# Reordering constants, weight loads and a flag in a graph kernel: three small moves on one Trainium2 core

## The chip, the cores and the metric

The kernel runs on one NeuronCore of a Trainium2 chip. The metric is the device time of one execution in microseconds (us). Below, TensorE is PE in profile lines (PEld its weight loads), VectorE is DVE, ScalarE is ACT, GpSimd is POOL, and SyncE is SP, whose queue (SPq) issues most transfers.

## The reference

The input is 16 graphs of 1024 nodes with 128 features, a 0/1 adjacency matrix for each, and a node mask of ones. Two layers are computed, each followed by a residual addition and a layer norm over the features. The first is a gated graph network (four steps of a GRU cell). The second first thins out each adjacency matrix row by row ("dilation"), then applies three rounds of neighbourhood averaging with batch norm, and a linear map of the three results:

```python
adj_d = _dilate(adj, mask)
def _sage(x, adj, Wr, Wx, b, mf):
    deg = jnp.clip(jnp.sum(adj, axis=-1, keepdims=True), 1.0, None)
    agg = jnp.einsum('bij,bjd->bid', adj, x) / deg
    out = agg @ Wr + x @ Wx + b
    return out / jnp.maximum(norm(out), 1e-12) * mf
h1 = _bn(relu(_sage(x,  adj_d, Wr1, Wx1, b1, mf)), g1, be1)
h2 = _bn(relu(_sage(h1, adj_d, Wr2, Wx2, b2, mf)), g2, be2)
h3 = _bn(relu(_sage(h2, adj_d, Wr3, Wx3, b3, mf)), g3, be3)
x = _layernorm(x + (concat([h1, h2, h3]) @ Wl + bl))
```

The batch norm takes its mean and variance over all graphs and nodes, so that each round has to be finished for all 16 graphs before the next one starts.

## The kernel before

The work stands in stages, and the order inside each stage is written out by hand: every engine runs its instructions in the order of the program, and semaphores join the engines.

From 0 to about 1330 us the GRU and the dilation run interleaved (`Gated` with lines L1062 to L1122, `FixPoint` with L735 to L912). The dilation is computed by a fixed number of sweeps instead of row by row; a check adds up, in the tile `bad`, whether that was enough and whether the inputs are what the fast path takes (0/1 values). At the very end `flagged` (L1954) reduces `bad` to one integer: VectorE takes the maximum over the columns, a matmul adds the partitions, and every engine loads the result into a register (`values_load`, L1967). If it is not zero, a general version of the whole computation runs (`tc.If`, L2007); with these inputs it is jumped over.

The first pass, `first` (L1415), takes the graphs one after the other in turns of 16 steps. `slot(b, t)` (L1600) is step t of the turn of graph b; in it the adjacency of graph b + 1 is already prepared. So there is a lead-in turn, b = -1, which only prepares graph 0. In a step, `unit` (L1474) turns one 128 x 512 piece of the thinned adjacency with matmuls (L1482, L1488, L1489) that read the loaded adjacency `p_a` and the removed entries `p_nr`; ScalarE writes the result to `p_at` (L1490), GpSimd packs it to bytes (`pack`, L1497) for the later passes, and VectorE checks the raw rows (`check`, L1506). `agg` (L1561) multiplies the features by `p_at`. `out_first` (L1570) applies the weights.

What the change moves in this pass:

- `load_given` (L1243) issues 20 transfers on the SP queue: six weight matrices and `Wl`, ten rows of vectors, the node mask three times. It is called at L1443, after the loads of graph 0 (two of `p_nr`, one of `p_s`, eight of `p_a`) and before the loop, so before the loads of graph 1, which `slot` issues at steps 4 to 11 of the lead-in turn: `p_nr` at 4 and 6, `p_s` at 7, the first four `p_a` tiles at 8 to 11. At step 10 the bytes of graph 0 are stored to `s_at`, after `pack` has written them. The transfers of the SP queue use eight semaphores in rotation, and an issue waits until the transfer eight places earlier has landed.
- `constants` (L1259), at step 9 of the lead-in turn, prepares small tiles on VectorE, among them `drop` (the identity with a changed first row) in the work tile `p_rl`, and a block of ones that three transfers store to `rho` (L1290).
- `first_weights` (L1293), at step 1 of the turn of graph 0, multiplies the first weight matrix by `drop`, turns the vectors and computes the bias row `s_r`, with PSUM tiles that TensorE writes and VectorE reads in alternation.

The second pass `second` (L1698) and the third pass `third` (L1830) compute rounds two and three from what the earlier pass stored. The third pass has 32 units (16 graphs, two halves) in a pipeline: in iteration i TensorE turns the rows of unit i - 3 (L1411), computes unit i (`out_next`, L1758, L1761, L1764), and VectorE and ScalarE scale and normalise the units in between.

`last` (L1867) adds the third linear map (L1890 to L1898) and does the final layer norm for each graph: eight tiles `u_y` of 128 x 128 are scaled and shifted, the first on GpSimd (L1921), the others on ScalarE (L1925), reading PSUM for tiles 4 to 7. For the last graph, VectorE takes tiles 2, 4 and 6 (L1923). Each graph is stored by one transfer of 512 KB on the SP queue (L1926).

Of the kernel before, what the change touches and what calls it, by code (L numbers as in the profile page):

```python
# [8 lines left out]
F32 = mybir.dt.float32  # L9
BF = mybir.dt.bfloat16  # L10
F16 = mybir.dt.float16
FR = mybir.dt.float32r
I32 = mybir.dt.int32
U8 = mybir.dt.uint8
AF = mybir.ActivationFunctionType
ALU = mybir.AluOpType
AX = mybir.AxisListType
# [4 lines left out]
P = 128  # L22
# [19 lines left out]
def rows_of(ap):  # L42

    return ap.rearrange("(k p) c -> p k c", p=P)
# [1152 lines left out]
class Sage:  # L1197
# [61 lines left out]
    def constants(self):  # L1259
# [16 lines left out]
        nc.vector.memset(self.r6[:, C:], 0.0)  # L1276
        work = self.wk.tile([P, NB, C], F32, name="p_rl", bufs=1)

        mask, junk = self.cst["mask"], work[:, 0, :].rearrange("p (a b) -> p a b", a=NB)
        nc.vector.scalar_tensor_tensor(junk, mask, 0.0, mask, op0=ALU.is_gt, op1=ALU.not_equal,  # L1280
                                       accum_out=self.bad[:, BAD - 1:BAD])

        drop = work[:, 1, :]
        nc.vector.tensor_copy(drop, ident)
        nc.vector.memset(drop[:1, :], -1.0)
        nc.vector.memset(drop[:1, :1], 0.0)
        o = work[:B, 4:, :].bitcast(BF).rearrange("p a b -> p (a b)")
        nc.vector.memset(o, 1.0)
        for i in range(3):
            nc.sync.dma_start(self.rho[:, 3 + i, :], o)  # L1290
        self.drop = drop

    def first_weights(self):  # L1293
        nc, ident = self.nc, self.cst["ident"]
        bank = lambda: self.ps1.tile([P, 4, P], F32, name="s_tr")[:, 0, :]
        w = bank()
        nc.tensor.matmul(w, self.drop, self.wr[:, 0, :], start=True, stop=True)
        nc.vector.tensor_copy(self.wr[:, 0, :], w)
        v = bank()[:, :10]
        nc.tensor.transpose(v, self.vr, ident[:10, :10])  # L1300
        nc.vector.tensor_copy(self.vt, v)
        self.weights(0, bank()[:6, :])
        nc.vector.tensor_copy(self.mask48, self.m48)
# [111 lines left out]
    def first(self):  # L1415

        nc, tc, cst = self.nc, self.tc, self.cst
        with ExitStack() as c:
# [22 lines left out]
            for k in range(4, NB):  # L1441
                self.load_a(0, k)
            self.load_given()  # L1443
            self.eps = self.const([P, 1], 1e-5, "s_eps")
# [4 lines left out]
            for t, v in ((self.xh, 1.0), (self.xl, 0.0)):  # L1449
                nc.vector.memset(t[:, :, :1].bitcast(F32), v)  # L1450
            for b in range(-1, B):
                for t in range(16):
                    self.slot(b, t)
# [146 lines left out]
    def slot(self, b, t):  # L1600
# [82 lines left out]
        if nxt:  # L1683
            if t == 10:
                nc.sync.dma_start(self.at8[n, 0], self.g[n]["b", 0])
            if t == 13:
                nc.sync.dma_start(self.x1[n], self.g[n]["s"])
        if (b, t) == (-1, 9):
            self.constants()
        if (b, t) == (0, 1):  # L1690
            self.first_weights()
# [138 lines left out]
    def third(self):  # L1830

        nc, tc = self.nc, self.tc
        with ExitStack() as c:
# [9 lines left out]
            units = [(b, f) for b in range(B) for f in range(2)]  # L1843
            for i in range(len(units) + 3):

                if i >= 3:
# [20 lines left out]
    def last(self, r48):  # L1867
        nc, tc, cst = self.nc, self.tc, self.cst
        with ExitStack() as c:
# [42 lines left out]
            def norm(b):  # L1912
                y, pp, mv, rs = st.pop(b)
                nc.vector.reciprocal(rs[:, 0, :], rs[:, 0, :])
                nc.vector.scalar_tensor_tensor(rs[:, 1, :], mv[:, :, 0], -1.0, rs[:, 0, :],
                                               op0=ALU.mult, op1=ALU.mult)
                for k in range(NB):
                    src = pp[:, k - 4, :] if k > 3 else y[:, k, :]
                    scale, shift = rs[:, 0, k:k + 1], rs[:, 1, k:k + 1]
                    if k == 0:  # L1920
                        nc.gpsimd.tensor_scalar(y[:, k, :], src, scale, shift, op0=ALU.mult, op1=ALU.add)  # L1921
                    elif b == B - 1 and k % 2 == 0:
                        nc.vector.tensor_scalar(y[:, k, :], src, scale, shift, op0=ALU.mult, op1=ALU.add)  # L1923
                    else:
                        nc.scalar.activation(y[:, k, :], src, AF.Identity, bias=shift, scale=scale)  # L1925
                nc.sync.dma_start(rows_of(self.out[b]), y)  # L1926

# [25 lines left out]

def flagged(tc, one, bad):  # L1954

    nc = tc.nc
    with tc.tile_pool(name="l_wk", bufs=1) as wk, tc.tile_pool(name="l_ps", bufs=1, space=PSUM) as ps:
        t = wk.tile([P, 1], F32, name="l_max")
        nc.vector.tensor_reduce(t, bad, axis=AX.X, op=ALU.max)
        nc.vector.tensor_scalar(t, t, 0.0, None, op0=ALU.not_equal)  # L1960
        col = wk.tile([P, 1], F32, name="l_col")
        nc.vector.memset(col, 1.0)
        pt = ps.tile([P, 1], F32, name="l_sum")
        nc.tensor.matmul(pt[:1], t, col, start=True, stop=True)
        f = one.tile([1, 1], I32, name="l_flag")
        nc.vector.tensor_scalar(f, pt[:1], 0.5, None, op0=ALU.is_gt)
    return nc.values_load(f[0:1, 0:1], min_val=0, max_val=1,  # L1967
                          skip_runtime_bounds_check_because="0 or 1 by is_gt")

# [19 lines left out]
def kernel(ctx: ExitStack, tc: tile.TileContext, x, adj, nodemask,  # L1989
# [7 lines left out]
    with ExitStack() as ctx:  # L1997
# [3 lines left out]
        with ExitStack() as c:  # L2001
# [3 lines left out]
            gru.run(fix.steps())  # L2005
        Sage(ctx, tc, cst, adj, not_r, summed, nodemask, W, vec, Wl, bl, out, bad).run()
    with tc.If(flagged(tc, one, bad) > 0):  # L2007
        general(tc, cst, x, adj, nodemask, weight, w_ih, w_hh, b_ih, b_hh, W, vec, Wl, bl, out)
# [31 lines left out]
```

## Time and profile before

| | |
|---|---|
| time, median of 3 runs | 2375.27 us (2373.47 to 2375.73) |
| span of the profiled execution | 2371.7 us |
| busy: PE, DVE, ACT, POOL | 2262.0 (95%), 1908.9 (80%), 1373.6 (58%), 1022.1 (43%) us |
| GRU and dilation | 0 to about 1330 us |
| first pass | about 1330 to 1870 us, 31 us a graph once it runs |
| third pass | about 2160 to 2282 us, 3.79 us a unit |
| last stage | about 2295 to 2362 us, then 9 us to the end of the span |

How to read it: the share of busy time is an average over stages. A TensorE that is busy 95% of the span is full in most stages, and the question for a change is in which stretch it stands, and for what. The timeline gives for each instruction its start, its duration, its engine and line, the tiles it writes and reads, and in brackets how long its engine was idle before it and what released it.

### The profile page before, as it was taken

The numbers are of one execution on the slowest core, as the hardware profiler recorded it, in microseconds if no ns is written. First come the engines' busy times: TensorE is split into PE (matmuls) and PEld (weight loads), VectorE is DVE, ScalarE is ACT, GpSimd is POOL, SyncE is SP. The second block draws the span as 40 slices with busy tenths as digits, with TensorE's granted clock in tenths as the row PEclk, the third lists the DMA queues.
The fourth block names the chain that finished last, engine by engine and source line by source line (L and its number), as shares of the span: only waits on it lengthen the run. The fifth ranks groups of instructions, "written<-read, shape, count | busy, mean of one in ns | idle before, by whom it ended". The sixth has DMA issues, their size and how long they took to land.

```text
span 2371.7 us, 35696 instructions
## 1 busy us (share of the span) xinstructions
PE 2262.0 (95%) x11929; PEld 1558.3 (66%) x11945; DVE 1908.9 (80%) x4130; ACT 1373.6 (58%) x3209; POOL 1022.1 (43%) x963
## 2 busy tenths in 40 slices
PE   6999999999999999999999699999999989999987
PEld 4665565666655656556566477777777768887865
DVE  4898998998989989989889877777777566665876
ACT  3656565656465655556564556656665545555756
POOL 3335254253362452533532446666666434441002
PEclk9999999999999999999999899999999999999999
DMA  7327245363353372543740677787778367774414
GB/s 263 112 97 263 72 163 177 115 216 129 119 201 108 115 248 68 198 142 115 234 133 25 236 279 274 270 297 278 273 272 298 116 237 247 246 247 157 138 43 135
DMA packets 214389, 436.17 MB, mean 184 GB/s; under 512 B 59570, under 2 KB 80724, under 8 KB 214196
## 3 DMA queue, kind: packets, MB, share of 16 engines
q1 hardware_dynamic: 186756, 345.96, 42.3%
q0 software_dynamic: 23040, 83.90, 10.4%
q10 hardware_dynamic: 4400, 3.95, 0.5%
q8 instruction: 96, 1.57, 0.3%
q14 instruction: 97, 0.79, 0.1%
HBM read 324.49 MB, written 109.25 MB: 183 GB/s over the span
## 4 chain that ended last, share of the span: by engine, by line
PE 63%; DVE 14%; DMA 8%; ACT 8%; issue 3%; POOL 3%; SPq 0%; DVEq 0%; ACTq 0%; POOLq 0%
PE h_g L1092 15%; PE h_g L1080 12%; PE p_ag L1561 9%; PE q_ag L1797 5%; PE q_ob L1764 3%; DVE f_rank L735 3%; DMA e_sum<-h_x 3%; PE p_u L1488 2%; PE p_u L1489 2%; DMA h_a<-in_adj_dram 2%; PE p_u L1482 2%; PE s_tr L1411 2%; ACT s_junk L1389 2%; PE q_oa L1758 2%; PE u_p L1890 1%
## 5 line engine op out<-in xcount | busy, mean ns | idle before, releaser
L1092 PE MATMUL h_g<-h_h,h_wh 128*128 128x512 f32 x768 | 397.7, 599 | 3.4 <-DVE h_r L1105 3.3
L1092 PE MATMUL h_g<-h_ms,h_wi 128*128 128x512 f32 x768 | 392.1, 592 | 0.0
L1497 POOL CAST p_b<-p_at 128x512 uint8<-128x512 f32 x256 | 252.5, 1006 | 137.5 <-ACT p_at L1490 129.5
L735 DVE TENSOR_TENSOR_SCAN f_rank<-f_a,f_first,f_pd 128x1024 f16<-128x1024 f32 x128 | 299.1, 2342 | 3.3
L1080 PE MATMUL h_g<-h_a,h_hi 128*128 128x512 f32 x1024 | 284.6, 418 | 6.6 <-DMA h_a<-in_adj_dram 6.6
L1490 ACT ACTIVATE p_at<-p_u,s_less 128x512 fp32r<-128x512 f32 x256 | 175.9, 688 | 157.5 <-PE p_u L1489 152.7
L1092 PEld LDWEIGHTS h_g<-h_ms,h_wi 128*128 128x128 f32 x768 | 145.6, 190 | 183.9 <-issue 161.6
L1121 POOL TENSOR_TENSOR h_h<-h_zh,h_r 128x512 f32<-128x512 f32 x126 | 181.9, 1443 | 194.9 <-DVE h_r L1120 172.8
L1080 PE MATMUL h_g<-h_a,h_lo 128*128 128x512 f32 x1024 | 264.2, 395 | 0.0
L1080 PEld LDWEIGHTS h_g<-h_a,h_hi 128*128 128x128 f32 x1024 | 188.4, 188 | 71.2 <-issue 20.1
L863 DVE SCALAR_TENSOR_TENSOR f_nr<-f_u,f_q,f_a 128x1024 bf16<-128x1024 f16 x128 | 184.0, 1454 | 56.9 <-ACT f_u L912 50.4
L1115 POOL TENSOR_TENSOR h_zh<-h_z,h_h 128x512 f32<-128x512 f32 x63 | 80.3, 1275 | 323.8 <-ACT h_z L1111 323.8
L1080 PEld LDWEIGHTS h_g<-h_a,h_lo 128*128 128x128 f32 x1024 | 190.0, 188 | 39.3
L1506 DVE SCALAR_TENSOR_TENSOR p_a<-p_a 128x1024 bf16<-128x1024 f32 x128 | 209.4, 1674 | 2.5 <-DMA p_a<-in_adj_dram 2.5
L1389 ACT ACTIVATE s_junk<-s_o 128x128 bf16<-128x128 f32 x384 | 113.8, 298 | 133.1 <-DVE s_o L1382 133.1
L1092 PEld LDWEIGHTS h_g<-h_h,h_wh 128*128 128x128 f32 x768 | 129.1, 190 | 86.6 <-issue 67.3
L1083 ACT COPY h_ms<-h_g 128x512 f32<-128x512 f32 x128 | 73.8, 577 | 175.4 <-PE h_g L1080 131.5
L1108 ACT ACTIVATE h_r<-h_r,h_bi 128x512 f32<-128x512 f32 x128 | 92.3, 721 | 138.5 <-DVE h_r L1107 138.5
L1488 PE MATMUL p_u<-ident_b,p_a 128*128 128x128 bf16 x1024 | 144.4, 221 | 13.8 <-DMA p_a<-in_adj_dram 12.8
L909 ACT ACTIVATE f_u<-f_rank,f_q 128x128 f16<-128x128 f16 (+7 forms) x128 | 110.6, 867 | 74.7 <-DVE f_rank L849 74.7
L1489 PE MATMUL p_u<-ident_b,p_nr 128*128 128x128 bf16 x1024 | 144.5, 221 | 0.0
L1764 PE MATMUL q_ob<-s_wxp,q_xt 128*128 128x256 f32 x512 | 130.5, 399 | 0.0
(258 smaller groups left out, 4936.0 us busy)
## 6 DMA issues: line engine op xcount, KB each, us to landing
h_a<-in_adj_dram POOLq DMA_DIRECT2D x128, 512.0 KB, 7.4
p_a<-in_adj_dram SPq DMA_DIRECT2D x128, 512.0 KB
f_a<-in_adj_dram SPq DMA_DIRECT2D x124, 512.0 KB
e_nr<-f_nr SPq DMA_DIRECT2D x128, 256.0 KB
p_nr<-e_nr SPq DMA_DIRECT2D x32, 1024.0 KB
s_at<-p_b SPq DMA_DIRECT2D x32, 512.0 KB
s_ag<-s_ag SPq DMA_DIRECT2D x64, 256.0 KB
q_agi<-s_ag SPq DMA_DIRECT2D x32, 512.0 KB
```

The source lines that it names most:

```text
L735: nc.vector.tensor_tensor_scan(out, a, other[:, 0, 0:1].to_broadcast([P, N]), start, op0=ALU.add, op1=ALU.bypass)
L863: nc.vector.scalar_tensor_tensor(nr, self.us[g], self.q[:, 2, g:g + 1], self.a[g], op0=ALU.not_equal, op1=ALU.is_ge)
L1080: nc.tensor.matmul(pm[f], part[:, j, :], st.adj[j][:, half[f]], start=(j == 0 and n == 0), stop=(j == NB - 1 and n == 1))
L1092: nc.tensor.matmul(pg, lhs, rhs, start=(i == 0), stop=(i == len(mm) - 1))
L1121: aid.tensor_tensor(h, zh, r, ALU.subtract)
L1488: nc.tensor.matmul(pu[:, i * P:(i + 1) * P], a[:, blk, 1], ib, start=False, stop=False)
L1489: nc.tensor.matmul(pu[:, i * P:(i + 1) * P], nr[:, k, blk], ib, start=False, stop=(i == 3))
L1490: nc.scalar.activation(g["at"][:, j, cols], pu, AF.Relu, bias=self.less2)
L1497: self.nc.gpsimd.tensor_copy(g["b", f][:, j, :], g["at"][:, j, f * HF:(f + 1) * HF].bitcast(F32))
L1506: self.nc.vector.scalar_tensor_tensor(low, a, 0.0, a, op0=ALU.is_gt, op1=ALU.not_equal, accum_out=self.bad[:, c:c + 1])
L1561: self.nc.tensor.matmul(pa, hi[:, j, :], at[:, j, f * HF:(f + 1) * HF], start=(start and n == 0), stop=(stop and n == len(js) - 1))
L1764: nc.tensor.matmul(pb[:, i], g["xt"][:, f, blk], self.wxp, start=False, stop=(i % 2 == 1))
```

## The change

It has three parts. The constants are prepared before the lead-in turn instead of in its step 9, in tiles that are free then (`wr2`, `wxp` and `mask48` instead of the work tile), and the weights' loads move from ahead of the turn to its step 11, behind the first loads of graph 1; the three stores of ones go to step 15 and `first_weights` to step 3 of the next turn. The flag is computed in iteration 8 of the third pass and loaded into registers in iteration 16, so that the end has no flag left to wait for. And the last graph's normalise is shared anew: GpSimd takes tiles 0 and 1, ScalarE tile 2, VectorE tiles 3 to 7, and the result is stored in two halves, one on the SP queue and one on ScalarE's queue. The aim is to let TensorE get the second graph's rows sooner, and to shorten what follows the last matmul.

```diff
--- before.py
+++ after.py
@@ -1274,27 +1274,22 @@
         nc.vector.tensor_add(self.graph, ident[:K, :B], ident[:K, B:2 * B])
         nc.vector.tensor_add(self.graph, self.graph, ident[:K, 2 * B:K])
         nc.vector.memset(self.r6[:, C:], 0.0)
-        work = self.wk.tile([P, NB, C], F32, name="p_rl", bufs=1)
-
-        mask, junk = self.cst["mask"], work[:, 0, :].rearrange("p (a b) -> p a b", a=NB)
+
+        mask, junk = self.cst["mask"], self.wxp[:, 0, :].rearrange("p (a b) -> p a b", a=NB)
         nc.vector.scalar_tensor_tensor(junk, mask, 0.0, mask, op0=ALU.is_gt, op1=ALU.not_equal,
                                        accum_out=self.bad[:, BAD - 1:BAD])
 
-        drop = work[:, 1, :]
+        drop = self.wr2
         nc.vector.tensor_copy(drop, ident)
         nc.vector.memset(drop[:1, :], -1.0)
         nc.vector.memset(drop[:1, :1], 0.0)
-        o = work[:B, 4:, :].bitcast(BF).rearrange("p a b -> p (a b)")
-        nc.vector.memset(o, 1.0)
-        for i in range(3):
-            nc.sync.dma_start(self.rho[:, 3 + i, :], o)
-        self.drop = drop
+        nc.vector.memset(self.mask48[:B, :], 1.0)
 
     def first_weights(self):
         nc, ident = self.nc, self.cst["ident"]
         bank = lambda: self.ps1.tile([P, 4, P], F32, name="s_tr")[:, 0, :]
         w = bank()
-        nc.tensor.matmul(w, self.drop, self.wr[:, 0, :], start=True, stop=True)
+        nc.tensor.matmul(w, self.wr2, self.wr[:, 0, :], start=True, stop=True)
         nc.vector.tensor_copy(self.wr[:, 0, :], w)
         v = bank()[:, :10]
         nc.tensor.transpose(v, self.vr, ident[:10, :10])
@@ -1440,7 +1435,6 @@
             self.load_s(0)
             for k in range(4, NB):
                 self.load_a(0, k)
-            self.load_given()
             self.eps = self.const([P, 1], 1e-5, "s_eps")
             self.less2 = self.const([P, 1], -2.0, "s_less2")
 
@@ -1448,6 +1442,7 @@
             self.xl = xp.tile([P, NB, C], FR, name="p_xl")
             for t, v in ((self.xh, 1.0), (self.xl, 0.0)):
                 nc.vector.memset(t[:, :, :1].bitcast(F32), v)
+            self.constants()
             for b in range(-1, B):
                 for t in range(16):
                     self.slot(b, t)
@@ -1685,9 +1680,13 @@
                 nc.sync.dma_start(self.at8[n, 0], self.g[n]["b", 0])
             if t == 13:
                 nc.sync.dma_start(self.x1[n], self.g[n]["s"])
-        if (b, t) == (-1, 9):
-            self.constants()
-        if (b, t) == (0, 1):
+        if (b, t) == (-1, 11):
+            self.load_given()
+        if (b, t) == (-1, 15):
+
+            for i in range(3):
+                nc.sync.dma_start(self.rho[:, 3 + i, :], self.mask48[:B, :])
+        if (b, t) == (0, 3):
             self.first_weights()
         if t == 1 and b >= 1:
             for f in range(2):
@@ -1842,6 +1841,12 @@
                 nc.sync.dma_start(self.ag[B - 1, f], last["ag", f])
             units = [(b, f) for b in range(B) for f in range(2)]
             for i in range(len(units) + 3):
+                if i == 8:
+                    pt = self.ps2.tile([P, 4, P], F32, name="s_tr")
+                    flag = flagged(nc, self.one, pt[:1, 0, :1], self.bad)
+                if i == 16:
+                    self.flag = nc.values_load(flag[0:1, 0:1], min_val=0, max_val=1,
+                                               skip_runtime_bounds_check_because="0 or 1 by is_gt")
 
                 if i >= 3:
                     b2, f2 = units[i - 3]
@@ -1917,13 +1922,17 @@
                 for k in range(NB):
                     src = pp[:, k - 4, :] if k > 3 else y[:, k, :]
                     scale, shift = rs[:, 0, k:k + 1], rs[:, 1, k:k + 1]
-                    if k == 0:
+                    if k == 0 or (b, k) == (B - 1, 1):
                         nc.gpsimd.tensor_scalar(y[:, k, :], src, scale, shift, op0=ALU.mult, op1=ALU.add)
-                    elif b == B - 1 and k % 2 == 0:
+                    elif b == B - 1 and k > 2:
                         nc.vector.tensor_scalar(y[:, k, :], src, scale, shift, op0=ALU.mult, op1=ALU.add)
                     else:
                         nc.scalar.activation(y[:, k, :], src, AF.Identity, bias=shift, scale=scale)
-                nc.sync.dma_start(rows_of(self.out[b]), y)
+                if b < B - 1:
+                    nc.sync.dma_start(rows_of(self.out[b]), y)
+                else:
+                    nc.sync.dma_start(rows_of(self.out[b])[:, 4:, :], y[:, 4:, :])
+                    nc.scalar.dma_start(rows_of(self.out[b])[:, :4, :], y[:, :4, :])
 
             row(0)
             row(1)
@@ -1951,21 +1960,17 @@
         self.last(r48)
 
 
-def flagged(tc, one, bad):
-
-    nc = tc.nc
-    with tc.tile_pool(name="l_wk", bufs=1) as wk, tc.tile_pool(name="l_ps", bufs=1, space=PSUM) as ps:
-        t = wk.tile([P, 1], F32, name="l_max")
-        nc.vector.tensor_reduce(t, bad, axis=AX.X, op=ALU.max)
-        nc.vector.tensor_scalar(t, t, 0.0, None, op0=ALU.not_equal)
-        col = wk.tile([P, 1], F32, name="l_col")
-        nc.vector.memset(col, 1.0)
-        pt = ps.tile([P, 1], F32, name="l_sum")
-        nc.tensor.matmul(pt[:1], t, col, start=True, stop=True)
-        f = one.tile([1, 1], I32, name="l_flag")
-        nc.vector.tensor_scalar(f, pt[:1], 0.5, None, op0=ALU.is_gt)
-    return nc.values_load(f[0:1, 0:1], min_val=0, max_val=1,
-                          skip_runtime_bounds_check_because="0 or 1 by is_gt")
+def flagged(nc, wk, pt, bad):
+
+    t = wk.tile([P, 1], F32, name="l_max")
+    nc.vector.tensor_reduce(t, bad, axis=AX.X, op=ALU.max)
+    nc.vector.tensor_scalar(t, t, 0.0, None, op0=ALU.not_equal)
+    col = wk.tile([P, 1], F32, name="l_col")
+    nc.vector.memset(col, 1.0)
+    nc.tensor.matmul(pt, t, col, start=True, stop=True)
+    f = wk.tile([1, 1], I32, name="l_flag")
+    nc.vector.tensor_scalar(f, pt, 0.5, None, op0=ALU.is_gt)
+    return f
 
 
 def general(tc, cst, x, adj, nodemask, weight, w_ih, w_hh, b_ih, b_hh, W, vec, Wl, bl, out):
@@ -2003,8 +2008,9 @@
             fix = FixPoint(c, tc, cst, adj, not_r, bad)
             c.enter_context(tc.manual_schedule(engines={ET.PE, ET.DVE, ET.Activation, ET.Pool, ET.SP}))
             gru.run(fix.steps())
-        Sage(ctx, tc, cst, adj, not_r, summed, nodemask, W, vec, Wl, bl, out, bad).run()
-    with tc.If(flagged(tc, one, bad) > 0):
+        sage = Sage(ctx, tc, cst, adj, not_r, summed, nodemask, W, vec, Wl, bl, out, bad)
+        sage.run()
+    with tc.If(sage.flag > 0):
         general(tc, cst, x, adj, nodemask, weight, w_ih, w_hh, b_ih, b_hh, W, vec, Wl, bl, out)
```

## The prediction

> **What bounds the kernel now.** I read the shares of the chain that ended last, then busy time by stage, then the timelines of the three places that the change touches: the turn ahead of the second graph, the third pass and the end.
>
> ```profile
> PE 63%; DVE 14%; DMA 8%; ACT 8%; issue 3%; POOL 3%; SPq 0%; DVEq 0%; ACTq 0%; POOLq 0%
> ```
>
> TensorE carries most of the chain. By stage (columns: the stretch, its length, busy microseconds of PE, PEld, DVE, ACT, POOL, granted clock, DMA share, GB/s):
>
> ```profile
> 1352.00:1368.00 16.00, 2.01 (x10) 0.93 (x11) 13.22 (x19) 0.55 (x2) 5.53 (x10) 0.66 0.86 309
> 1368.00:1405.00 37.00, 34.87 (x271) 27.25 (x271) 26.78 (x69) 20.36 (x49) 17.49 (x19) 0.96 0.63 240
> 1405.00:1436.00 31.00, 30.51 (x255) 24.27 (x254) 23.00 (x59) 18.84 (x47) 19.60 (x19) 1.00 0.80 298
> ```
>
> In the first pass TensorE is full (30.5 of 31 us a graph), except for one hole of 16 us ahead of the first turn. Any microsecond of that hole comes off the end. TensorE's timeline there, with the idle time and its releaser in brackets:
>
> ```profile
> 1353.16 0.39 PE L1482 MATMUL p_u<-p_nr,ident_b 128*128 128x512 bf16 x1 [1.35 <-DMA p_nr<-e_nr]
> 1358.96 0.29 PE L1488 MATMUL p_u<-ident_b,p_a 128*128 128x128 bf16 x1 [5.41 <-DMA p_a<-in_adj_dram]
> ...
> 1365.01 0.29 PE L1488 MATMUL p_u<-ident_b,p_a 128*128 128x128 bf16 x1 [4.43 <-DMA p_a<-in_adj_dram]
> ...
> 1367.56 0.29 PE L1488 MATMUL p_u<-ident_b,p_a 128*128 128x128 bf16 x1 [2.16 <-DMA p_a<-in_adj_dram]
> ```
>
> It waits for the second graph's `p_nr` and its four adjacency tiles, one after the other. The load queue shows why they are late:
>
> ```profile
> 1328.07 0.59 SPq L1248 DMA_DIRECT2D s_wr<-in_L_gnn_Wr_dram  x1
> ...
> 1347.18 0.97 SPq L1466 DMA_DIRECT2D p_nr<-e_nr  x2
> 1348.20 0.50 SPq L1472 DMA_DIRECT2D p_s<-e_sum  x1
> 1348.82 1.20 SPq L1458 DMA_DIRECT2D p_a<-in_adj_dram  x2
> 1359.14 1.25 SPq L1290 DMA_DIRECT2D s_rho<-p_rl  x3
> ```
>
> From 1328 to 1347 the queue works through 20 small loads of weights, paced by earlier transfers; then it stops from 1350 to 1359 at the `s_rho` stores, which wait for VectorE's memset of their source. The third and fourth adjacency tile stand behind that. VectorE is late by one row:
>
> ```profile
> 1352.38 5.30 DVE L1284 COPY p_rl<-ident 128x128 f32<-128x128 f32 x1
> ```
>
> The third pass has no slack at all: each unit of 3.79 us is TensorE back to back, and VectorE's last work on a unit comes after TensorE has left it:
>
> ```profile
> 2191.83 0.60 PE L1411 MATMUL s_tr<-ident,s_r 128*128 128x128 f32 x4
> ...
> 2192.47 0.69 DVE L1382 TENSOR_TENSOR s_o<-q_ob,s_o 128x512 f32<-128x512 f32 x1 [0.72 <-PE s_tr L1411]
> 2193.08 0.68 DVE L1864 TENSOR_TENSOR s_acc<-q_ob,s_acc 128x512 f32<-128x512 f32 x1
> ```
>
> At the end the flag comes after the last normalise (chain, in order of time), and then its load:
>
> ```profile
> 2361.29 0.42 DVE u_y L1923
> 2361.71 0.02 issue
> 2361.73 0.47 ACT u_y L1925
> 2362.20 0.04 issue
> 2362.24 0.20 PE l_sum L1964 x2
> ```
>
> [...]the copy above lasts from 1352.38 to 1357.68, just while GpSimd's casts run (to 1357.6); the PSUM copy of the same shape at L1298 takes 0.29. [...]Here eight L1561 matmuls take 3.43 us after the hole and 2.07 later. [...]Here SP's branch is at 2363.2 and its next instruction at 2367.9.
>
> **The change, part by part.**
>
> *Constants before the lead-in turn.* Some 15 VectorE rows, about 3 us[...]. In the new order ten stand between the two L1058 additions, where VectorE idles 1.37 us, the others behind them, where it idles 4.34 us for `p_s`. GpSimd is all but idle there[...]. Cost nothing, hidden by the wait for `p_s`.
>
> *Weights behind the second graph's rows.* The two `p_nr` and `p_s` now take the queue slots that the weights had, from 1328. The first three adjacency tiles wait for their buffers (unit 7, done at 1344.4; checks to 1344.2). The fourth stands behind the `s_at` store of the first graph, which waits for GpSimd's eighth cast. That one is the first of two casts from 1348.15 (3.37 us together), so about 1349.8, and the fourth tile is issued at about 1350.3. Bandwidth: the transfers run at about 420 GB/s until 1341, and then 2.1 (`p_nr`) + 0.5 (`p_s`) + 2.1 (tiles) + 0.5 (store) = 5.2 MB follow, 12.4 us, to 1353.4[...]: TensorE resumes at 1355.4 instead of 1367.6, a gain of 12.2. Bounds: not before unit 15 is done (1352.0), and not later than 1357.6 (issue at 1351.5 and the 6.1 us that this tile took before).
>
> What is given back: VectorE used the hole for constants and six checks. Now six checks of 1.3 to 1.8 us (8 to 11 us) start at 1351, so it enters the turn 2 to 5 us further behind TensorE than before (resume + 3.4 then). `first_weights` moves from step 1 to step 3, where its two PSUM round trips queue behind four `p_s` normalisations (1.25 us) on VectorE; on TensorE it holds steps 4 and 5, and it cost 1.6 us before. I take 2.7 us in all (0.5 to 5). The weights land by about 1361, before step 3 (about 1364). Net of this part: -9.5.
>
> *Flag in the third pass.* At unit 8 the flag's matmul is put ahead of the turn and needs the reduce, which is behind VectorE's `s_acc` of unit 7. From the rows above: TensorE is free at 2191.83, `s_acc` ends at 2193.76, the reduce (0.27) and compare (0.15) with handovers end at about 2194.3, the matmul takes 0.2: 2.65 us in which TensorE stands, with all later units behind it. At unit 16 each engine loads the register, 0.46 to 0.55 us by its rows at the end; VectorE and ScalarE have slack (busy 32.8 and 31.4 of 40 us from 2200 to 2240), TensorE has none: 0.5 to 1.0 with its waits, I take 0.75. Sum +3.4 (2 to 4, or 6 if the clock drops as it did after a hole of 3.07 us at 2156.8, where the first unit took 6.3 instead of 3.35).
>
> *The end.* ScalarE keeps one of four tiles of the last graph and is done at 2360.05 + 0.45 = 2360.5; VectorE takes five, from 2358.1 to about 2360.0; GpSimd two, to 2359.2. Both half stores are issued by about 2360.9 instead of 2362.3, and the flag's 0.3 and the load's 0.5 us are gone: the branches start about 2.1 us earlier (2361.1 instead of 2363.2). GpSimd branches earlier still, and its drain of 2.85 us, the last long row, moves with it. But the data of two graphs' outputs flow at 340 GB/s, and those end only 0.6 us earlier. I take -2.5 (0.6 to 3.5).
>
> Sum: -9.5 + 3.4 - 2.5 = -8.6; 2375.3 - 8.6 = 2366.7 us.
>
> **Rivals.** (1) *The hole closes with little given back*: resume at 1353 to 1354, the clock stays up (1.4 us less for the first matmuls), VectorE catches up: -13.5 + 3 - 3 = -13.5, 2361.8. For it: VectorE has 8 us of slack a turn. Against: the `s_at` store ahead of the fourth tile. (2) *VectorE or the queue becomes the bound in the second turn*, and half the gain goes: -5 + 3.5 - 2 = -3.5, 2371.8. For it: the checks, the weights and `first_weights` crowd into 15 us. Against: the four later tiles are needed only 22 us after the resume. (3) *Slower*: the hole is filled but the first turn is stretched as much (gain 2 or less), the stall in the third pass drops the clock (+6) and the end is bound by its transfers (-1): 2375.3 - 2 + 6 - 1 = 2378.3. Against it: 12 us of waiting on named transfers, whose cause is taken away.
>
> **How the numbers follow.** Forecast 0.55, rival 1 0.22, rival 2 0.18, rival 3 0.05. Range 2360.5 to 2371.5: it takes in rival 1 and most of rival 2 at its lower end. 0.2% is 4.75 us, so faster is below 2370.5: the forecast nearly whole, rival 1, a fifth of rival 2: 0.82. Within: most of rival 2, a little of the forecast: 0.14. Slower: 0.04.
>
> **What would show it.** Right: `p_a` waits of TensorE around 1353 to 1356 sum to under 4 us, the L1284 copy takes 0.3 us, one TensorE gap of 2 to 3 us at unit 8 with the flag matmul behind the reduce, a last branch about 2 us after the last activation. Wrong: `p_a` waits at 1360 or later; TensorE waits on VectorE or ScalarE in the turn after it that sum to over 5 us; half-clock rows behind the flag; the final drains still following the output's landing.

## The result, and the profile after

| | before | after |
|---|---|---|
| time, median | 2375.5 us | 2364.74 us (2360.16 to 2367.58) |
| span of the profiled execution | 2371.7 us | 2363.2 us |

The time before is the median of 4 runs here. The ratio is 0.9952, 95% interval 0.9933 to 0.9971: 10.8 us faster, where 8.6 were forecast. Timed a second time (e9), the ratio was 0.9956 (0.9938 to 0.9973).

To see where the time went I cut each trace at the same four instructions: the last addition of the GRU (VectorE, L1058); the first `p_ag<-p_at,p_xh` matmul of the first pass (TensorE has the whole of graph 0); the first `p_ag<-p_at,p_rh` of graph 1, from where on all kernels run alike; and the last `u_p` matmul. The last columns are the 32 units with what follows them up to that matmul, and what comes after it to the end of the span. All are differences of starts, in us; the two averages count from the GRU's end:

| kernel | GRU ends at | to graph 0's first average | to graph 1's `p_rh` average | third pass and last stage | last matmul to end |
|---|---|---|---|---|---|
| before | 1330.16 | 37.56 | 95.66 | 192.75 | 16.1 |
| after | 1325.77 | 25.80 | 86.28 | 201.57 | 12.95 |
| after, again (e9) | 1325.51 | 25.79 | 87.85 | 201.22 | 12.98 |

Four amounts, then: the lead-in part gains 9.4 us (7.8 in e9), the third pass and the last stage lose 8.8, the end gains 3.2, and the GRU, which no edit touches, ends 4.4 us sooner. The rest, from graph 1's `p_rh` to the third pass, is 737.0 and 736.6 us. Some 2 of the 8.8 us belong to this one trace of before: the four other kernels with the old third pass (e1, e3, e5, e10) take 194.0 to 194.8 us there, not 192.75.

Two figures given for the kernel before are wrong, though nothing below rests on them: a graph of the first pass takes 33.7 us once it runs (its averages start at 1405.3 and 1439.0 us), not 31, and the last `p_ag` matmul starts at 1899.5 us, so the pass ends near 1900, not 1870.

**The gap.** TensorE's timeline after, at the place of the 16 us gap (start, duration, engine, line; in brackets the idle time before it and what ended it):

```profile
1347.25 0.38 PE L1477 MATMUL p_u<-p_nr,ident_b 128*128 128x512 bf16 x1 [0.27 <-ACT p_at L1485]
1348.92 0.23 PE L1483 MATMUL p_u<-ident_b,p_a 128*128 128x128 bf16 x1 [0.41 <-DMA p_a<-in_adj_dram]
1351.47 0.23 PE L1483 MATMUL p_u<-ident_b,p_a 128*128 128x128 bf16 x1 [2.27 <-DMA p_a<-in_adj_dram]
```

The four longest waits, 13.35 us together, have become two of 2.7, and the fourth adjacency tile is the only one left that counts. The load queue shows why:

```profile
1323.94 5.34 SPq L1461 DMA_DIRECT2D p_nr<-e_nr  x2
1330.00 5.06 SPq L1467 DMA_DIRECT2D p_s<-e_sum  x1
1340.34 1.29 SPq L1453 DMA_DIRECT2D p_a<-in_adj_dram  x3
1346.13 0.33 SPq L1680 DMA_DIRECT2D s_at<-p_b  x1
1346.56 0.37 SPq L1453 DMA_DIRECT2D p_a<-in_adj_dram  x1
1346.98 0.77 SPq L1248 DMA_DIRECT2D s_wr<-in_L_gnn_Wr_dram  x1
...
1357.35 1.72 SPq L1688 DMA_DIRECT2D s_rho<-s_mask  x3
```

`p_nr` goes out 23 us earlier than before (19 when counted from the GRU's end); three tiles follow in one go; the fourth stands behind the `s_at` store; weights and the ones for `rho` come last. How 20 small loads could hold the rows so long shows in the queue's own waits in the profile before: the second `s_wr` waits 3.6 us for the `p_nr` eight places ahead of it, and the second `s_wx` 1.0 for the `p_s` eight places ahead. The constants now run beside an idle GpSimd, and the copy that took 5.30 us takes 0.22:

```profile
1326.59 0.22 DVE L1283 COPY s_wr<-ident 128x128 f32<-128x128 f32 x1
```

By stage (length, then busy us of PE, PEld, DVE, ACT, POOL, clock, DMA share, GB/s):

```profile
1336.00:1352.00 16.00, 12.69 (x127) 9.49 (x127) 16.00 (x23) 10.60 (x18) 15.11 (x12) 0.91 1.00 365
1352.00:1389.00 37.00, 33.09 (x254) 25.49 (x253) 28.83 (x72) 18.53 (x46) 23.94 (x23) 0.95 0.74 260
1389.00:1420.00 31.00, 30.56 (x247) 24.08 (x247) 22.99 (x60) 19.24 (x47) 19.72 (x20) 1.00 0.81 287
```

The 16 us ahead of graph 0's first average held 2.0 us of TensorE work before and hold 12.7 now, with the transfer engines full (share 1.00). The 37 us behind them hold 33.1 instead of 34.9: here some of the gain is given back.

**The flag.** TensorE in the third pass after:

```profile
2173.49 1.99 PE L1763 MATMUL q_ob<-s_wxp,q_xt 128*128 128x256 f32 x8
...
2177.28 1.99 PE L1763 MATMUL q_ob<-s_wxp,q_xt 128*128 128x256 f32 x8
2181.24 0.19 PE L1970 MATMUL s_tr<-l_col,l_max 128*1 128x1 f32 x2 [1.97 <-DVE l_col L1969]
2181.36 0.66 PE L1406 MATMUL s_tr<-ident,s_r 128*128 128x128 f32 x4
2181.86 1.67 PE L1757 MATMUL q_oa<-s_wr,q_agi 128*128 128x128 f32 x8
2183.46 1.03 PE L1760 MATMUL q_ob<-s_r,q_rho 6*128 6x256 bf16 x4
2184.41 3.78 PE L1763 MATMUL q_ob<-s_wxp,q_xt 128*128 128x256 f32 x8
2187.99 1.06 PE L1406 MATMUL s_tr<-ident,s_r 128*128 128x128 f32 x4
```

The wait is 1.97 us; with the matmul behind it 2.25, where 2.65 were forecast. But the eight matmuls behind it take 3.78 us instead of 1.99: the clock has dropped (0.57 granted from 2182 to 2190 us, 1.00 before and after). From one L1763 group to the next it is 7.13 and then 6.01 us instead of 3.79 each, 5.55 us lost: 2.25 for the stall, 3.3 for the clock.

**The end.** The branch on the flag and what follows it, before (minimum/median/maximum in ns, first and last start):

```profile
L2007 SPq EVENT_SEMAPHORE  x8: 17/17/17, 2367.9 to 2368.4; - x8
...
L2007 POOLq COMPARE_BRANCH  x1: 45/45/45, 2363.2 to 2363.2; - x1
L2007 SPq COMPARE_BRANCH  x1: 50/50/50, 2363.2 to 2363.2; - x1
L2007 PEldq COMPARE_BRANCH  x1: 3850/3850/3850, 2363.2 to 2363.2; - x1
...
L2007 POOLq EVENT_SEMAPHORE  x1: 17/17/17, 2368.0 to 2368.0; - x1
```

and after:

```profile
L2013 SPq EVENT_SEMAPHORE  x8: 17/17/17, 2361.1 to 2361.6; - x8
L2013 PEldq COMPARE_BRANCH  x1: 4679/4679/4679, 2348.0 to 2348.0; - x1
...
L2013 POOLq COMPARE_BRANCH  x1: 45/45/45, 2354.2 to 2354.2; - x1
...
L2013 SPq COMPARE_BRANCH  x1: 50/50/50, 2357.1 to 2357.1; - x1
L2013 POOLq EVENT_SEMAPHORE  x1: 17/17/17, 2357.4 to 2357.4; - x1
```

Before, all engines branch at the same moment, and each needs 4 to 5 us to its next instruction. GpSimd's drain of 2.85 us follows only then. After, each engine branches when its own work is done: TensorE and GpSimd go through this beside the last normalise and the stores, and SP's branch, with 4.0 us to its next instruction, is what is left at the end.

### The profile page after: what moved, and what is told of

The parts are those of the page before. It is cut to its first block, busy times and chain, and to the rows that moved or that the text cites. A ratio compares the mean times of both kernels' runs of the same rounds, so it can differ in the third digit from the quotient of the medians.

```text
span 2363.2 us, 35730 instructions
## 1 busy us (share of the span) xinstructions
PE 2271.6 (96%) x11945; PEld 1565.0 (66%) x11945; DVE 1905.2 (81%) x4132; ACT 1372.9 (58%) x3206; POOL 1029.3 (44%) x964
## 5 line engine op out<-in xcount | busy, mean ns | idle before, releaser
L1492 POOL CAST p_b<-p_at 128x512 uint8<-128x512 f32 x256 | 257.6, 1026 | 120.7 <-ACT p_at L1485 112.8
L1080 PE MATMUL h_g<-h_a,h_hi 128*128 128x512 f32 x1024 | 284.4, 418 | 4.9 <-DMA h_a<-in_adj_dram 4.8
L1121 POOL TENSOR_TENSOR h_h<-h_zh,h_r 128x512 f32<-128x512 f32 x126 | 181.6, 1441 | 194.8 <-DVE h_r L1120 172.7
L1080 PE MATMUL h_g<-h_a,h_lo 128*128 128x512 f32 x1024 | 265.4, 396 | 0.0
L1080 PEld LDWEIGHTS h_g<-h_a,h_hi 128*128 128x128 f32 x1024 | 188.4, 188 | 68.8 <-issue 20.1
L1080 PEld LDWEIGHTS h_g<-h_a,h_lo 128*128 128x128 f32 x1024 | 190.6, 189 | 39.5
L1763 PE MATMUL q_ob<-s_wxp,q_xt 128*128 128x256 f32 x512 | 133.0, 404 | 0.0
```

The costliest lines, as they stand in the source:

```text
L1080: nc.tensor.matmul(pm[f], part[:, j, :], st.adj[j][:, half[f]], start=(j == 0 and n == 0), stop=(j == NB - 1 and n == 1))
L1121: aid.tensor_tensor(h, zh, r, ALU.subtract)
L1492: self.nc.gpsimd.tensor_copy(g["b", f][:, j, :], g["at"][:, j, f * HF:(f + 1) * HF].bitcast(F32))
L1763: nc.tensor.matmul(pb[:, i], g["xt"][:, f, blk], self.wxp, start=False, stop=(i % 2 == 1))
```

## The experiments

All ratios are to the kernel before, with 95% intervals. Its median was 2375.7 us beside e1 to e4, 2375.4 beside e5 to e8, 2374.6 beside e9 to e12.

**One part at a time: e1, e2, e3.** e1 has only the constants and the weights' loads; e2 only the flag in the third pass; e3 only the last normalise and its two stores. Each is the diff above without the other hunks.

> Only the first part of the change (constants and weights' loads). From the two traces: TensorE's start on the aggregation of the second graph less the start of the lead-in turn shrinks by 11.8 us, and 2.4 us come back in the turn after it, so if the parts simply add, the kernel ends 9.4 us earlier: 2366 us. A rival, that the whole change's gain is this part's and the other two cancel, gives the same 2364 to 2365 as the whole change.

> Only the flag moved into the third pass, the rest as before. Stall and clock: TensorE stands 2.2 us at unit 8 for the reduce behind VectorE's work on unit 7, and then runs at half clock (3.3 us more); at the end 0.6 to 0.9 us are saved: 4.7 to 4.9 us slower, 2380. If the stall alone is the mechanism and the slow clock in the trace was chance: 1.5 us slower, 2377. If the register load counts on TensorE: 0.5 to 1 us more than either.

> Only the last normalise shared anew and stored in two halves, flag at the end as before. If the end is set by ScalarE's tiles and what follows: 1.5 to 2.5 us faster, 2373.5.[...]

| kernel | time, us | ratio | GRU ends at | to graph 1's `p_rh` | third pass and last stage | last matmul to end |
|---|---|---|---|---|---|---|
| e1 | 2363.58 | 0.995 (0.9935 to 0.9964) | 1329.80 | 85.67 | 194.20 | 16.1 |
| e2 | 2373.81 | 0.9989 (0.9979 to 1.0) | 1328.43 | 97.96 | 198.75 | 12.6 |
| e3 | 2374.96 | 0.9997 (0.9989 to 1.0005) | 1329.06 | 96.23 | 194.69 | 15.3 |

e1 is as fast as the whole change, close to what the rival had. The other two parts together bring nothing beside it. Alone, the flag wins 3.5 us at the end and loses about 4.3 in the third pass (the two groups of `q_ob<-s_wxp,q_xt` around it start 8.06 us apart instead of 3.79; the half clock is shorter here, 3.4 us, than in the changed kernel, 6.8). The new sharing wins 0.8 us in its trace, where 1.5 to 2.5 were to come if ScalarE's tiles set the end, and in the time nothing that is clear of the noise. I had expected e2 to be slower, and it is not: I had counted the stall, but not what the flag's move brings at the end, nor a shorter GRU that comes with it (see "What no step foresaw"). The end's gain comes from the flag and not from the sharing: e2, with the old sharing and one store, is 0.4 us shorter there than the changed kernel.

**The flag without its stall: e4.** The changed kernel, with the reduce four iterations ahead of the matmul that uses it:

```diff
+                if i == 4:
+                    worst, col = flag_columns(nc, self.one, self.bad)
                 if i == 8:
                     pt = self.ps2.tile([P, 4, P], F32, name="s_tr")
-                    flag = flagged(nc, self.one, pt[:1, 0, :1], self.bad)
+                    flag = flag_sum(nc, self.one, pt[:1, 0, :1], worst, col)
```

> The whole change, but with the flag's reduce four units ahead (unit 4) of its matmul (unit 8). If the stall comes from the reduce standing behind VectorE's work on the unit before, TensorE no longer waits, the clock stays up, and 5.5 us come off the changed kernel: 2359. If the stall comes from the matmul's PSUM bank, or from the matmul itself, nothing changes: 2364 to 2365.

Measured: 2359.59 us, ratio 0.9933 (0.9919 to 0.9947); third pass and last stage 194.91 instead of 201.57. The flag's matmul has no wait, and the unit behind it starts 4.06 us after the one ahead. The intervals of the two times overlap a little; it is the traces that show the cause. By stage (busy us of PE, clock, DMA share, GB/s), the changed kernel:

```profile
2178.00:2182.00 4.00, 2.03 (x14) 1.00 0.52 175
2182.00:2190.00 8.00, 8.00 (x34) 0.57 0.13 47
2190.00:2200.00 10.00, 10.00 (x62) 1.00 0.48 111
```

and e4:

```profile
2178.00:2182.00 4.00, 4.00 (x28) 1.00 0.75 227
2182.00:2190.00 8.00, 8.00 (x52) 1.00 0.45 132
2190.00:2200.00 10.00, 10.00 (x67) 1.00 0.39 123
```

In the 8 us after the stall, TensorE is busy throughout both times, but does 34 instructions at clock 0.57 instead of 52 at 1.00. A busy share alone would have hidden this.

**Which move fills the gap: e5 and e10.** e5 moves only the constants (and their stores of ones, at step 9), e10 only the weights' loads (with `first_weights` at step 3).

```diff
 e5, against e1
+            self.load_given()
-        if (b, t) == (-1, 11):
-            self.load_given()
-        if (b, t) == (-1, 15):
+        if (b, t) == (-1, 9):
             for i in range(3):
                 nc.sync.dma_start(self.rho[:, 3 + i, :], self.mask48[:B, :])
-        if (b, t) == (0, 3):
+        if (b, t) == (0, 1):
             self.first_weights()

 e10, against e1
-            self.constants()
-        if (b, t) == (-1, 15):
+        if (b, t) == (-1, 9):
+            self.constants()
             for i in range(3):
                 nc.sync.dma_start(self.rho[:, 3 + i, :], self.mask48[:B, :])
```

> Only the constants ahead of the lead-in turn (and the ones' stores at its step 9, with nothing to wait for); weights' loads stay ahead of the second graph's rows, flag and end as before. If the gap had two causes in series (the weights' loads ahead of the rows, and the stores of ones that wait for VectorE ahead of the third and fourth tile), this removes the second alone: the fourth tile is issued about 8 us earlier than in the kernel before and TensorE resumes some 6 to 8 us earlier, of which 1 to 2 us are given back: about 2370 us. If the weights' loads alone made the rows late, the gain is under 2 us: 2374 us or more. If the constants alone did it, it is as fast as both moves together (2363.6 us).

> Only the weights' loads behind the second graph's rows (and their use in step 3 of the next turn); constants and the stores of ones stay in step 9 of the lead-in turn, flag and end as before. If the gap has two causes in series, the stores of ones still wait for VectorE until about 1358 us and the third and fourth tile stand behind them: TensorE resumes 2 to 3 us earlier at most, and the time is about 2 us below before: 2373.5. If the two moves simply add, what the constants alone left over is gained here: -12.1 + 3.6 = -8.5, 2367.

Measured: e5 2371.86 us, ratio 0.9987 (0.9981 to 0.9994); e10 2370.48 us, 0.9982 (0.9975 to 0.9988). Alone they gain 3.6 and 4.1 us, together 12.1 (e1). From the GRU's end to graph 0's first average it is 35.08 us in e5 and 32.78 in e10, against 37.56 before and 25.46 in e1; to graph 1's `p_rh` the traces gain 1.1 and 3.0 us alone, 10.0 together. So the two causes do stand in series, and a good part of the gain, 4.4 of 12.1 us by the times and 5.9 of 10.0 by the traces, comes only with both moves. The sizes that I had expected were off: TensorE resumes 2.5 us earlier in e5, not 6 to 8, and 4.8 earlier in e10, not 2 to 3. What is left over is what each leaves in place. In e10, TensorE stands once, for long:

```profile
1349.08 0.38 PE L1476 MATMUL p_u<-p_nr,ident_b 128*128 128x512 bf16 x1 [0.27 <-ACT p_at L1484]
1357.67 0.29 PE L1482 MATMUL p_u<-ident_b,p_a 128*128 128x128 bf16 x1 [7.33 <-DMA p_a<-in_adj_dram]
1360.61 0.29 PE L1482 MATMUL p_u<-ident_b,p_a 128*128 128x128 bf16 x1 [2.54 <-DMA p_a<-in_adj_dram]
```

for the two tiles behind the stores of ones, which its queue issues at 1351.95 us, when VectorE has written them. In e5 the queue starts the rows late:

```profile
1344.14 0.97 SPq L1462 DMA_DIRECT2D p_nr<-e_nr  x2
1345.15 0.50 SPq L1468 DMA_DIRECT2D p_s<-e_sum  x1
1345.78 1.17 SPq L1454 DMA_DIRECT2D p_a<-in_adj_dram  x2
```

20 us later than after, because the weights stand ahead of them. I was wrong on a detail of e10: its constants come a little earlier, so that the copy runs ahead of GpSimd's next casts (from 1350.49 us) and takes 0.21 us, and the stores waited until 1352, not 1358. The long instruction isn't gone: the row check behind the constants (L1500, at 1351.86) takes 4.93 us where the next ones take 1.3, while GpSimd works until 1355.6. It only stands behind the stores now.

**What gives part of it back: e6, e7, e12.** Between graph 0's first average and graph 1's `p_rh`, before takes 58.10 us, after 60.48. TensorE waits there after for `p_rl` (0.78), `s_rdeg` (0.64) and `s_wr` (0.96; 0.39 before), 2.0 us more than before (1.7 over all waits), and is busy 0.7 us longer. e6 takes four checks off VectorE ahead of these waits:

```diff
-            if t >= 12:
+            if t >= 12 and now:
                 self.check(n + 1, t - 12)
+            if b == 0 and 6 <= t < 10:
+                self.check(n, t - 6)
```

> The changed kernel with four of VectorE's row checks moved from steps 12 to 15 of the lead-in turn to steps 6 to 9 of the turn after it. If VectorE is what makes TensorE give back 2.4 us of the filled gap in that turn, TensorE's waits on VectorE and ScalarE between the resume and the next turn fall from about 3 us to under 1.5, and the time is about 2 us below the changed kernel (2362.7 us). If the loads of the weights or the half clock give it back, no difference beyond 0.5 us and the same waits.

Measured: 2359.34 us, ratio 0.9931 (0.9919 to 0.9944), but the stage is no shorter: 86.43 us from the GRU to graph 1's `p_rh`. VectorE's second batch of statistics, at 1359.55 us in the changed kernel, is done early in e6, and then VectorE stands:

```profile
1349.38 0.35 DVE L1512 BATCH_NORM_AGGREGATE p_mv<-p_st 128x2 f32<-128x6 f32 x4
1354.41 0.20 DVE L1516 RECIPROCAL p_rs<-p_rs 128x8 f32<-128x8 f32 x1 [4.68 <-ACT p_rs L1515]
```

TensorE's waits remain, 4.0 us over all: `s_wr` 0.93, `s_rdeg` 0.25 and 1.13. The wait for `p_rl` is gone from this turn, but stands, 0.81 us long, at the start of the next, behind the checks that were moved there (their statistics start at 1392.76 us). So e6 moved VectorE's load rather than took it away. That the round trips between engines give the time back is argued from the waits that remain, and not shown. The lower time of e6 isn't explained by this stage: its profile has the earliest end of the GRU of all (1323.13 us), and was taken of one of its two longest executions (2363.3 us). Executions of one kernel spread this much, and the shortest of e6 and of the changed kernel had a higher mean granted clock than the longest: e6 2357.1 us at 0.989 and 2365.0 at 0.986, the changed kernel 2360.16 at 0.989 and 2367.58 at 0.985.

e7 stores the first graph's bytes behind the weights, so that the fourth tile doesn't wait for them:

```diff
-            if t == 10:
+            if t == 10 and now:
                 nc.sync.dma_start(self.at8[n, 0], self.g[n]["b", 0])
+            if t == 12 and not now:
+                nc.sync.dma_start(self.at8[n, 0], self.g[n]["b", 0])
```

> The changed kernel with the first graph's byte store behind the weights' loads (step 12 instead of 10), so that the fourth adjacency tile doesn't stand behind it. TensorE waits 2.3 us for that tile in the changed kernel. If this wait is on the path, the time falls by about 2.3 us (2362.5 us). If VectorE bounds the turn behind it, TensorE resumes earlier by 2 us and waits that much longer for VectorE: under 1 us gained.

Measured: 2361.32 us, ratio 0.9934 (0.992 to 0.9948). The wait for the tile falls to 1.0, the first average comes 1.2 us sooner after the GRU (24.60), and graph 1's `p_rh` 1.4 us later (87.68). TensorE's waits in this stretch (total, times, longest):

```profile
PE s_tr L1549 <- ACT p_rl L1542: 4.1, 1, 4.1
PE p_u L1483 <- DMA p_a<-in_adj_dram: 1.0, 1, 1.0
```

Here VectorE does bound: its checks run to 1359.6 us, the statistics and ScalarE's root come behind them, and `p_rl` behind that root. A wait taken from the path came back, larger, one stage on. The median is still 3.4 us below the changed kernel's, which the stage doesn't explain; the profile is of the longest of its six executions (2356.14 to 2366.02 us).

**The end with one store: e8.** e4 with the new sharing, but the old single store:

```diff
-                if b < B - 1:
-                    nc.sync.dma_start(rows_of(self.out[b]), y)
-                else:
-                    nc.sync.dma_start(rows_of(self.out[b])[:, 4:, :], y[:, 4:, :])
-                    nc.scalar.dma_start(rows_of(self.out[b])[:, :4, :], y[:, :4, :])
+                nc.sync.dma_start(rows_of(self.out[b]), y)
```

> The kernel of e4 (changed kernel, flag's reduce four iterations earlier) with the last graph stored by one transfer on the SP queue, the new sharing kept. In the changed kernel SP's half store takes 1.71 us to issue beside ScalarE's half store, and SP's branch is behind it. If that issue sets the end, SP branches about 1.3 us earlier, and from the last matmul to the end it is about 11.3 us instead of 12.95: 2358 us against 2359.6. If the landing of the data sets it, one transfer of 512 KB issued at the same moment ends no earlier: 12.9 us or more.

Measured: 2359.55 us, ratio 0.9932 (0.992 to 0.9945); 12.57 us from the last matmul to the end: exactly what e2 has with the old sharing, though ScalarE is done 1.7 us earlier. Two halves take 12.95. Both theories miss. SP branches no sooner with one store (7.0 us after the last matmul, 6.9 with two halves), and its next instruction comes 3.3 us behind the branch instead of 4.0. The last store's issue takes 1.78 us as a single one too, where the others take 0.37:

```profile
L1933 SPq DMA_DIRECT2D out_dram<-u_y x16: 372/372/1782, 2297.9 to 2350.1; - x16
```

It goes out half a microsecond after the store of the graph ahead of it (2349.56). In e2, with data ready later, the issue takes 0.37 us, and SP branches at about the same distance, 7.1. Being close behind another store doesn't explain the long issue alone: in e3 a half store goes out just as close (0.46 us) behind another and takes 0.54:

```profile
L1929 SPq DMA_DIRECT2D out_dram<-u_y x1: 535/535/535, 2363.0 to 2363.0; - x1
```

In e8 the other four engines have branched by then, in e3 none has. Whether that is the reason wasn't tried; the cause is open.

**Together: e9, e11, e12.** e9 is the changed kernel again. e11 joins the edits of e4, e6, e7 and e8. e12 is e11 with `first_weights` ahead of step 3's normalisations.

> The changed kernel once more, so that it stands beside the kernel before and the three below on one chip. Its profile lies 4.4 us ahead of the kernel before at the end of the GRU, which the change doesn't touch. If that lead is chance, the stage itself comes out nearer to before here, and the time is that of the terms seen in the traces, -9.5 (gap) + 5.6 (flag) - 3.2 (end) = -7.1, so 2368; if the lead belongs to the kernel, 2364.

> e4, e6, e7 and e8 together: the flag's reduce at iteration 4, four checks of VectorE in the turn after, the first graph's bytes stored behind the weights' loads, one output store. The trace of e7 says that TensorE resumes 1.2 us earlier and then waits 4.1 us for VectorE's checks; with these moved away (e6) that wait goes: from the last GRU addition to the second graph's average 84.5 us instead of 86.3, then no stall at unit 8 and 12.6 us from the last matmul to the end: 2 us below e4, 2357.5. If the first turn is bound by round trips and not by these, it equals e4 (2359.6).

> e11 with the first round's weights prepared ahead of the four p_s normalisations of step 3 instead of behind them. TensorE waits 0.96 us there for VectorE's copy of s_wr, 0.39 in the kernel before. If the round trips behind these normalisations give back part of the gain, that wait falls to about 0.4 and the turn is 0.5 us shorter; otherwise the wait moves to another line and the turn is as long as in e11.

| kernel | time, us | ratio | to graph 0's first average | to graph 1's `p_rh` | third pass and last stage | to end |
|---|---|---|---|---|---|---|
| e9 | 2364.47 | 0.9956 (0.9938 to 0.9973) | 25.79 | 87.85 | 201.22 | 12.98 |
| e11 | 2355.89 | 0.9922 (0.9908 to 0.9936) | 24.21 | 84.36 | 194.99 | 12.4 |
| e12 | 2355.89 | 0.9919 (0.9904 to 0.9935) | 24.56 | 85.94 | 195.15 | 12.4 |

e11 beats both kernels: 18.7 us below before, 8.6 below the changed kernel beside it. The stage came out as expected (84.36 us, 84.5 forecast): with e6's edit, the wait of 4.1 us for `p_rl` that e7's had brought is gone from this turn. That is 1.6 us below e4 (85.97), 1.9 and 3.5 below the changed kernel. The times of e11 and e4 differ by 3.7 us, but their intervals overlap, and e12, with the same two edits, has 85.94: that the two edits help each other is likely, not shown. In e12 the wait for `s_wr` falls to 0.38 and another grows, in the waits of TensorE:

```profile
PE s_tr L1406 <- DVE s_rdeg L1551: 2.4, 2, 2.2
```

so nothing is gained. All waits together are 0.25 us shorter than in e11; the turn is longer because the half clock lasts 6.8 us of it instead of 3.4.

## Why the prediction was right, and where not

- **The lead-in, -9.5.** Right: -9.4 in the first trace, -7.8 in the second (e9). TensorE's first average came 11.8 us sooner in both (12.2 forecast, in which the 2 us between the last bytes at 1353.4 and TensorE's start at 1355.4 were my assumption, taken from no profile), and 2.4 and 4.0 us were given back (2.7 forecast); the difference of the two traces is the half clock, 3.4 us of the turn in the first and 6.8 in e9. Waits for `p_a` sum to under 4 us (2.7), the fourth tile does stand behind the `s_at` store. The constants cost nothing, as forecast; the copy takes 0.22 us beside an idle GpSimd (0.21 in e10, ahead of its casts) and took 5.30 while casts ran. The reason given for the loss, VectorE's lag and the later `first_weights`, is neither confirmed nor refuted as a whole: TensorE does wait for `p_rl` behind VectorE's checks (0.78 us, 1.61 in e9) and for `s_wr` and `s_rdeg` in step 3, but e6 and e12 only moved such waits to other places.
- **The flag in the third pass, +3.4.** The step that failed in size: it cost 5.55 us at units 8 and 9. The stall of 2.65 measured 2.25. The register load of 0.75 measured nothing: TensorE's load is at 2212.3 us and takes 489 ns, and the units around it start 3.79 us apart, like the others. The clock drop, put only at the edge of the range and half-clock rows behind the flag among the signs of being wrong, is what happened: 3.3 us. The four kernels with the stall and all parts take 201.3 us in third pass and last stage, the eight without it (all others but before and e2) 194.7: 6.6 in all. Of the 1.0 us beyond the 5.55, 0.7 lie in the last stage, from its first `u_p` matmul to its last: 61.6 us against 60.9. In all 14 profiles this stretch, less the time that the half clock takes from it, is 58.6 us; the half clock that begins between third pass and last stage only reaches further into it in these four (3.0 us taken, 2.1 to 2.6 in the eight).
- **The end, -2.5.** -3.2, but only in part for the reason given. The new sharing and the two halves were to bring the earlier store and a branch 2.1 us earlier: SP branches 0.8 us earlier, counted from the last matmul, and with the flag gone the two halves cost 0.4. The flag's move alone brought 3.5 (e2): 0.6 by SP's earlier branch, the rest behind it, since GpSimd's drain no longer starts at the very end, which the prediction had named, and SP's next instruction comes 3.4 us behind its branch instead of 4.7, for a reason that is open.
- **What no step foresaw.** The GRU ends 4.4 us earlier after. Eight profiles of kernels with all three parts have it at 1323.1 to 1327.1 us (mean 1325.2), six with one part or none at 1326.9 to 1330.2 (mean 1328.7). Counted from TensorE's first L1080 matmul (34.84 us before, 33.83 after, 36.66 in e2), so without the start of the program, the GRU takes 1290.2 to 1292.4 us in the nine kernels with the flag moved, e2 among them, and 1293.7 to 1295.4 in the five without. So some 3.4 us come with the flag's part, in a stage whose code is the same, and TensorE idles 3.0 us less there (15.4 against 18.4 us on average). e9's expectation that this was chance fell. How the edit brings it is open.

So -9.4 + 6.6 - 3.2 - 3.4 = -9.4, near the 10.8 and 10.1 measured; the terms are from single traces, and the first is 1.6 us smaller in e9. The flag's loss, 3 us larger than forecast, and the GRU's unexpected gain cancel, and that is luck; without the second, the time would have been about 2368 to 2370, still in the range. The rival of a closed gap with little given back came near in time (2361.8), but not in its mechanism. That VectorE binds the second turn is true of e7, and of the changed kernel for 0.8 to 1.6 us only. That the stall would drop the clock stood in the rival that ended slower; this part of it was the true one.

## What to carry to other kernels

Read a gap as a queue, not as a wait: two things stood in one load queue ahead of the rows, and each move alone brought a third of the time that both brought. Before a small reduction goes into a full pipeline, ask how far back its input can be computed: four iterations turned a loss of 5.5 us into one of 0.3. And a scalar that decides a branch is best read long before the branch: here engines that were done could then branch beside those that were not, TensorE at 2348.0 us and SP at 2357.1 instead of both at 2363.2, and the flag's move alone made the end 3.5 us shorter (e2).

## What the hardware showed that I had not expected

- The clock dropped behind an idle time of TensorE of 1.97 us (2.33 in e2) in each kernel with the stall; in the changed kernel it was 0.57 over the next 8 us, in e2 the half clock lasted 3.4 us. In the changed kernel a gap of 2 us cost more through the clock (3.3 us) than by itself (2.25), in e2 less (about 1.7). The length of the gap alone doesn't decide it: a gap of 1.71 us near the end of the first pass (ahead of `p_ag<-p_at,p_rh`) is in all 14 profiles, and the clock drops behind it in five (the changed kernel, where the next eight matmuls take 3.55 us, e9, e3, e8, e11) and stays up in nine (before among them, where they take 2.11). In the profiles before and after, the stretches at half clock that ended within the profile lasted 3.41, 6.83, 10.24 or 13.65 us.
- A register load of 489 ns on TensorE in the full third pass cost nothing that the units show (3.79 us apart with it and without).
- The branch over the general version held TensorE's sequencer for 3.85 us before, 4.68 after and 5.53 in e3, and SP's next instruction came 4.7 us behind its branch before, 4.0 after and 3.4 in e2; why was not shown.
- The issue of a 512 KB store took 1.78 us instead of 0.37 in e8, close behind another one; why is open (0.54 for a half store as close behind another in e3).
